# Part of the stores moved from SyncE's queue to ScalarE's

## The chip, the cores and the metric

The kernel runs on one core of a Trainium2 chip. The metric is the device time of one execution in microseconds; before the change it was 1874.4 us (median of two runs, 1874.36 and 1874.45). The core has five engines, each with its own stream of instructions: TensorE (PE, matmul), VectorE (DVE), ScalarE (ACT), GpSimd (POOL) and SyncE (SP). Here SyncE only issues DMA transfers. ScalarE can issue them too.

## The reference

The inputs are `xi` and `xj`, each 1024 samples x 39 rows x 16 numbers. For each pair of rows c < r (741 pairs) the outer product of row r of `xj` with row c of `xi` is formed, normalised over samples and elements (one mean and one variance per pair), scaled and shifted by `gamma` and `beta`, and multiplied by a 16 x 16 matrix W:

```python
cross = xj[:, rows, :, None] * xi[:, cols, None, :]          # 1024 x 741 x 16 x 16
mean = jnp.mean(cross, axis=(0, 2, 3), keepdims=True)
var = jnp.mean(jnp.square(cross - mean), axis=(0, 2, 3), keepdims=True)
normed = (cross - mean) * jax.lax.rsqrt(var + BN_EPS)
normed = normed * gamma[None, :, None, None] + beta[None, :, None, None]
out = normed[:, :, None, :, :] * W[None, None, :, :, :]
```

The output is 1024 x 741 x 256 float32, 777 MB; the inputs are 5 MB.

## The kernel before

128 partitions hold 8 samples each (NT = 8). From Gram sums the kernel first works out a scale s and a shift t for every pair, so that the output is (x * s + t) * W. Then it goes through 152 tiles. A tile is one row r with its r pairs, for T = 2 of the 8 samples. The first four tiles are row 19, the next eight alternate between rows 20 and 18. Then come the rows 38 down to 21, each together with the short row 38 - r (38 stands alone), so that a long and a short tile always fill 76 places of the buffer `y_sb`. That buffer has room for two such fillings, used in turn (`slot`).

```python
mid = (F - 1) // 2                                            # 19
tiles = [(mid, t0, t0 // T * half // 2) for t0 in range(0, NT, T)]
slot = 0
for r in (mid + 1, *range(F - 1, mid + 1, -1)):
    for t0 in range(0, NT, T):
        tiles.append((r, t0, slot * half))
        if r < F - 1:
            tiles.append((F - 1 - r, t0, slot * half + T * r))
        slot ^= 1
```

`products(n)` forms the outer products of tile n into `y_sb`: 32 instructions (2 samples x 16 numbers of `xj`), most on ScalarE, the rest on GpSimd. For rows of 7 and less (OUTER = 7) they are formed by GpSimd, and for 4 and less by VectorE, without ScalarE.

```python
for t in range(T):
    for i in range(E):
        product(n, nc.scalar if i < split else nc.gpsimd, t, i, xs[:, t])
```

`finish(n)` adds t and multiplies by W in place. VectorE does one instruction for each pair and both samples; a few pairs are GpSimd's (in rows over 33 ScalarE does the first half of that share). It is here that the stores are issued, piece by piece, as pairs become finished:

```python
for t in range(0, T, size):                                   # size = 2 from tile 2 on
    for c0, c1 in zip(bounds(n), bounds(n)[1:]):
        for c in [*range(c0, min(c1, p0)), *range(max(c0, p1), c1)]:
            stt(y[:, t : t + size, c, :], y[:, t : t + size, c, :],
                t_sb[:, n0 + c : n0 + c + 1], w_dve.to_broadcast([P, size, EE]), ALU.add, ALU.mult)
        store(n, c0, c1, t, t + size)

def store(n, c0, c1, t_from=0, t_to=T):
    r, t0, _ = tiles[n]
    n0 = first[r]
    whole = n >= len(FIRST_PIECES) and r <= WHOLE             # 8 entries; WHOLE = 36
    step = 1 if r > mid and (whole or c1 == r) else t_to - t_from
    for t in range(t_from, t_to, step):
        if whole and step == 1 and t == t_to - 1:
            if c1 < r:
                continue
            c0 = 0
        nc.sync.dma_start(
            out_v[:, t0 + t : t0 + t + step, (n0 + c0) * EE : (n0 + c1) * EE],
            view(n)[:, t : t + step, c0:c1, :].rearrange("p t n e -> p t (n e)"))
```

`bounds(n)` gives one piece for rows up to 30 and two above. So a long row up to 30 is stored as two transfers (one for each sample), a row of 31 to 36 as three (two pieces of the first sample, then the second sample whole), rows 37 and 38 as three (the first piece of both samples in one transfer, then the last piece of each sample), and a short row as one.

The loop puts the instructions into each engine's stream in this order:

```python
for n in range(1, len(tiles)):
    if n + 2 < len(tiles):
        scale_xi(n + 2)                                       # GpSimd: xi times s
    finish(n)
    ...
    if n + 1 < len(tiles):
        products(n + 1)
    ...
```

Of the kernel before, what the change touches and what calls it, by code (L numbers as in the profile page):

```python
# [14 lines left out]
T = 2  # L15
# [4 lines left out]
FIRST_PIECES = (  # L20
    (0, 1, 3, 6, 10, 14, 19), (0, 4, 9, 14, 19), (0, 4, 11, 19), (0, 9, 19), (0, 10, 20), (0, 9, 18), (0, 10, 20), (0, 9, 18)
)
# [10 lines left out]
OUTER, POOL_I_BESIDE = 7, 3  # L33
# [10 lines left out]
def tile_pair_outer_batchnorm(  # L44
# [15 lines left out]
    nc = tc.nc  # L60
# [3 lines left out]
    EE = E * E  # L64
# [7 lines left out]
    tiles = [(mid, t0, t0 // T * half // 2) for t0 in range(0, NT, T)]  # L72
# [25 lines left out]
    out_v = out.rearrange("(p t) o n i j -> p t (o n i j)", t=NT)  # L98
# [44 lines left out]
    def view(n):  # L143
        r, _, u = tiles[n]
        return y_sb[:, u : u + T * r, :].rearrange("p (t n) e -> p t n e", t=T)

    def product(n, engine, t, i, src):

        r, t0, _ = tiles[n]
        y = view(n).rearrange("p t n (i j) -> p t n i j", j=E)[:, t, :, i, :]  # L150
        scale = xj_sb[:, t0 + t, r, i : i + 1]
        if engine is nc.scalar:
            nc.scalar.activation(y, src, AF.Copy, scale=scale)  # L153
        else:
            engine.tensor_scalar(y, src, scale, 1.0, ALU.mult, ALU.mult)  # L155
# [13 lines left out]
    def scale_xi(n):  # L169
        r, t0, _ = tiles[n]  # L170
        if r <= SHORT:
            return
        n0 = first[r]
        xs = scaled.tile([P, T, r, E], F32, tag="xs", name=f"xs_{r}_{t0}")
        nc.gpsimd.tensor_tensor(  # L175
            xs,
            xi_sb[:, t0 : t0 + T, 0:r, :],
            s_sb[:, :, n0 : n0 + r, :].to_broadcast([P, T, r, E]),
            ALU.mult,
        )  # L180
        xs_of[n] = xs

    def products(n):

        r, t0, _ = tiles[n]
        if r <= SHORT:
            xs = scaled_short.tile([P, T, r, E], F32, tag="xs_short", name=f"xs_{r}_{t0}")
            nc.vector.tensor_tensor(
                xs,
                xi_sb[:, t0 : t0 + T, 0:r, :],  # L190
                s_short[:, first[r] : first[r] + r]
                .unsqueeze(1)
                .unsqueeze(3)
                .to_broadcast([P, T, r, E]),
                ALU.mult,
            )
            for t in range(T):
                nc.vector.tensor_tensor(  # L198
                    view(n)[:, t].rearrange("p n (i j) -> p n i j", j=E),
                    xs[:, t].unsqueeze(2).to_broadcast([P, r, E, E]),  # L200
                    xj_short[:, t0 + t, r - 1 : r, :].unsqueeze(3).to_broadcast([P, r, E, E]),
                    ALU.mult,
                )
            return
        xs = xs_of.pop(n)
        if r <= OUTER:
            for t in range(T):
                nc.gpsimd.tensor_tensor(  # L208
                    view(n)[:, t].rearrange("p n (i j) -> p n i j", j=E),
                    xs[:, t].unsqueeze(2).to_broadcast([P, r, E, E]),  # L210
                    xj_sb[:, t0 + t, r : r + 1, :].unsqueeze(3).to_broadcast([P, r, E, E]),
                    ALU.mult,
                )
            return
        if n < 3:
            split = E - POOL_I_FIRST[n]
        elif r > LONG:
            split = E - POOL_I_LONG
        else:
            split = E - (POOL_I_BESIDE if SHORT < F - 1 - r <= OUTER else POOL_I)  # L220
        for t in range(T):
            for i in range(E):
                product(n, nc.scalar if i < split else nc.gpsimd, t, i, xs[:, t])

    def store(n, c0, c1, t_from=0, t_to=T):
        r, t0, _ = tiles[n]
        n0 = first[r]

        whole = n >= len(FIRST_PIECES) and r <= WHOLE
# [3 lines that stand above are left out]
                if c1 < r:  # L233
                    continue
                c0 = 0
            nc.sync.dma_start(  # L236
                out_v[:, t0 + t : t0 + t + step, (n0 + c0) * EE : (n0 + c1) * EE],
                view(n)[:, t : t + step, c0:c1, :].rearrange("p t n e -> p t (n e)"),
            )

    def affine(n, pairs, engines=(nc.scalar, nc.gpsimd)):

# [11 lines left out]
    def weigh(n):  # L254

        y = view(n)
        for c0, c1 in zip(bounds(n), bounds(n)[1:]):
            affine(n, range(c0, min(c1, OWN)), (nc.vector,))
            nc.vector.tensor_tensor(  # L259
                y[:, :, c0:c1, :],  # L260
                y[:, :, c0:c1, :],
                w_dve.unsqueeze(1).to_broadcast([P, T, c1 - c0, EE]),
                ALU.mult,
            )
            store(n, c0, c1)
# [10 lines left out]
    def finish(n):  # L276


        r = tiles[n][0]
        n0 = first[r]  # L280
        y = view(n)
        long = r > LONG
        p1 = r // 2 if long else r
        if long:
            share = POOL_PAIRS_LONG
        elif RAW < n < 10:
            share = POOL_PAIRS_FIRST
        else:
            share = int(r * POOL_SHARE + 0.5) if r > SHORT else 0
        p0 = p1 - share  # L290
        step = POOL_PAIRS_LONG // 2 if long else r
        for c0 in range(p0, p1, step):
            c1 = min(c0 + step, p1)
            for c in range(c0, c1):
                t_c = t_sb[:, n0 + c : n0 + c + 1]
                if long:
                    nc.scalar.activation(y[:, :, c, :], y[:, :, c, :], AF.Identity, bias=t_c)  # L297
                else:
                    nc.gpsimd.tensor_scalar(  # L299
                        y[:, :, c, :], y[:, :, c, :], t_c, 1.0, ALU.add, ALU.mult  # L300
                    )
            nc.gpsimd.tensor_tensor(  # L302
                y[:, :, c0:c1, :],
                y[:, :, c0:c1, :],
                w_sb.unsqueeze(1).to_broadcast([P, T, c1 - c0, EE]),
                ALU.mult,
            )

        size = 1 if n == RAW else T
        for t in range(0, T, size):  # L310
            for c0, c1 in zip(bounds(n), bounds(n)[1:]):
                for c in [*range(c0, min(c1, p0)), *range(max(c0, p1), c1)]:
                    stt(  # L313
                        y[:, t : t + size, c, :],
                        y[:, t : t + size, c, :],
                        t_sb[:, n0 + c : n0 + c + 1],
                        w_dve.to_broadcast([P, size, EE]),
                        ALU.add,
                        ALU.mult,
                    )  # L320
                store(n, c0, c1, t, t + size)

    with tc.manual_schedule():
# [121 lines left out]
        for n in range(len(steps)):  # L445
# [12 lines left out]
            t0 = steps[n][0]  # L458
# [72 lines left out]
        def apply(group):  # L531
            ps, n0, n1 = spread_of[group]
            nc.vector.tensor_mul(ps[:, 1], ps[:, 1], st_sb[:, 0, n0:n1])
            if group == SHORT_GROUP:

                nc.vector.tensor_mul(ps[:, 0], ps[:, 0], st_sb[:, 0, n0:n1])
                nc.vector.tensor_copy(st_sb[:, 0, n0:n1], ps[:, 0])
            else:
                nc.vector.tensor_mul(st_sb[:, 0, n0:n1], ps[:, 0], st_sb[:, 0, n0:n1])
            nc.vector.tensor_add(st_sb[:, 1, n0:n1], ps[:, 1], st_sb[:, 1, n0:n1])  # L540
# [15 lines left out]
        for n in range(1, len(tiles)):  # L556
            if n + 2 < len(tiles):
                scale_xi(n + 2)
            finish(n)
            for group, (_, _, _, tile_of) in enumerate(ROW_GROUPS):  # L560
                if n == tile_of:
                    apply(group)
            if n + 1 < len(tiles):
                products(n + 1)
            if n == 12:
                nc.scalar.copy(xj_short, xj_sb[:, :, 1 : SHORT + 1, :])

# [27 lines left out]
```

## Time and profile before

| Engine | busy | share of the span | instructions |
|---|---|---|---|
| VectorE | 1723.0 us | 92% | 2641 |
| ScalarE | 1584.7 us | 85% | 3152 |
| GpSimd | 1552.0 us | 83% | 1650 |
| DMA, queue q1 | - | 98.2% of 16 engines | 53344 packets |

The span is 1873.1 us. The page of the profile gives the busy time of each engine, then the span in 40 slices of 46.8 us with the busy share of each in tenths, then the DMA queues. The groups below those say for one line of code and one engine how many instructions there were, their busy time in all, the mean of one, and after the second bar how long the engine was idle just before them and for what (the "releaser"). `out<-in` are names of the program, with the shapes (partitions x elements). "SPq" and "ACTq" are the parts of SyncE and ScalarE that issue transfers. A mean of one instruction includes its overlap with the next, so that a row of instructions takes a little less than count times mean.

Short rows are stored in one transfer of 256 KB for each pair, long rows at 128 KB for each pair and sample. From issue to landing a store took 2.3 us at the least, 18.4 us in the median and 27.8 us at the most.

### The profile page before, as it was taken

The numbers are of one execution on the slowest core, as the hardware profiler recorded it, in microseconds if no ns is written. First come the engines' busy times: TensorE is split into PE (matmuls) and PEld (weight loads), VectorE is DVE, ScalarE is ACT, GpSimd is POOL, SyncE is SP. The second block draws the span as 40 slices with busy tenths as digits, with TensorE's granted clock in tenths as the row PEclk, the third lists the DMA queues.
The fourth block names the chain that finished last, engine by engine and source line by source line (L and its number), as shares of the span: only waits on it lengthen the run. The fifth ranks groups of instructions, "written<-read, shape, count | busy, mean of one in ns | idle before, by whom it ended". The sixth has DMA issues, their size and how long they took to land. (4 is left out here: it accounts for less than half of the span.)

```text
span 1873.1 us, 9236 instructions
## 1 busy us (share of the span) xinstructions
PE 26.0 (1%) x130; PEld 23.2 (1%) x130; DVE 1723.0 (92%) x2641; ACT 1584.7 (85%) x3152; POOL 1552.0 (83%) x1650
## 2 busy tenths in 40 slices
PE   5000000000000000000000000000000000000000
PEld 4000000000000000000000000000000000000000
DVE  8999888899999999999999999999999999999994
ACT  8999888898888877666799999999899998989892
POOL 9999877787777788999988888888888888888882
DMA  5999999999999999999999999999999999999998
GB/s 210 390 422 422 428 426 424 427 425 424 428 424 427 425 429 422 427 425 425 417 435 425 426 431 427 424 431 426 426 431 426 430 426 429 427 428 427 428 426 355
DMA packets 54711, 783.61 MB, mean 418 GB/s; under 512 B 4720, under 2 KB 6384, under 8 KB 17520
## 3 DMA queue, kind: packets, MB, share of 16 engines
q1 hardware_dynamic: 53344, 779.72, 98.2%
q10 hardware_dynamic: 1296, 3.29, 0.5%
q14 instruction: 70, 0.57, 0.1%
q8 instruction: 1, 0.02, 0.0%
HBM read 6.00 MB, written 776.99 MB: 418 GB/s over the span
## 5 line engine op out<-in xcount | busy, mean ns | idle before, releaser
L313 DVE SCALAR_TENSOR_TENSOR y_sb<-y_sb,st_sb,w_dve 128x512 f32<-128x512 f32 (+1 forms) x2511 | 1653.1, 738 | 114.5 <-issue 99.1
L153 ACT ACTIVATE y_sb<-xs,xj_sb 128x144 f32<-128x144 f32 (+23 forms) x2930 | 1453.4, 587 | 239.1 <-DMA out_dram<-y_sb 207.7
L302 POOL TENSOR_TENSOR y_sb<-y_sb,w_sb 128x2048 f32<-128x2048 f32 (+3 forms) x155 | 517.7, 3345 | 90.0 <-ACT y_sb L297 80.4
L155 POOL TENSOR_SCALAR y_sb<-xs,xj_sb 128x320 f32<-128x320 f32 (+19 forms) x1006 | 558.3, 581 | 9.1 <-DMA out_dram<-y_sb 9.0
L175 POOL TENSOR_TENSOR xs<-xi_sb,st_sb 128x640 f32<-128x640 f32 (+33 forms) x135 | 184.1, 1363 | 179.2 <-ACT y_sb L153 174.6
L299 POOL TENSOR_SCALAR y_sb<-y_sb,st_sb 128x512 f32<-128x512 f32 x291 | 197.1, 694 | 5.1 <-ACT y_sb L153 5.1
L297 ACT ACTIVATE y_sb<-y_sb,st_sb 128x512 f32<-128x512 f32 x160 | 100.2, 709 | 3.9 <-POOL y_sb L155 2.2
L208 POOL TENSOR_TENSOR y_sb<-xs,xj_sb 128x1280 f32<-128x1280 f32 (+2 forms) x24 | 66.7, 2803 | 0.0
L198 DVE TENSOR_TENSOR y_sb<-xs,ps 128x256 f32<-128x256 f32 (+3 forms) x32 | 24.8, 818 | 0.5
L522 PE MATMUL ps<-y_sb 38*128 38x38 f32 (+37 forms) x76 | 16.4, 397 | 2.8 <-DVE y_sb L508 2.8
L522 PEld LDWEIGHTS ps<-y_sb 38*128 38x128 f32 x76 | 16.3, 329 | 3.1 <-DVE y_sb L508 3.1
L379 ACT ACTIVATE y_sb<-y_sb 128x1216 f32<-128x1216 f32 x8 | 9.7, 1211 | 2.9 <-POOL y_sb L368 2.6
L153 ACT ACTIVATE y_sb<-xi_sb,xj_sb 128x304 f32<-128x304 f32 x24 | 11.4, 538 | 0.0
L384 DVE TENSOR_REDUCE y_sb<-y_sb 128x76 f32<-128x1216 f32 (+1 forms) x9 | 10.9, 1268 | 0.0
L259 DVE TENSOR_TENSOR y_sb<-y_sb,w_dve 128x2048 f32<-128x2048 f32 (+4 forms) x6 | 10.7, 1840 | 0.1
L368 POOL TENSOR_TENSOR y_sb<-xi_sb,y_sb 128x1216 f32<-128x1216 f32 x4 | 9.0, 2262 | 1.2 <-DMA xi_sb<-in_r_xi_dram 1.0
L358 DVE TENSOR_REDUCE y_sb<-xi_sb 128x38 f32<-128x608 f32 (+1 forms) x6 | 5.9, 988 | 3.9 <-DMA xi_sb<-in_r_xi_dram 3.9
L368 POOL TENSOR_TENSOR y_sb<-xj_sb,y_sb 128x1216 f32<-128x1216 f32 x4 | 9.0, 2264 | 0.0
L252 POOL TENSOR_SCALAR y_sb<-y_sb,st_sb 128x512 f32<-128x512 f32 x8 | 6.4, 817 | 2.5 <-ACT y_sb L153 2.5
L404 PE MATMUL ps<-y_sb 128*38 128x77 f32 x48 | 8.1, 337 | 14.0 <-DVE y_sb L384 13.8
L358 DVE TENSOR_REDUCE y_sb<-xj_sb 128x38 f32<-128x608 f32 (+1 forms) x6 | 5.9, 990 | 1.3 <-DMA xj_sb<-in_r_xj_dram 1.3
L250 ACT ACTIVATE y_sb<-y_sb,st_sb 128x512 f32<-128x512 f32 x9 | 6.5, 801 | 0.2 <-ACT y_sb L153 0.2
(60 smaller groups left out, 42.8 us busy)
## 6 DMA issues: line engine op xcount, KB each, us to landing
out_dram<-y_sb SPq DMA_DIRECT2D x16, 3072.0 KB, 21.7
out_dram<-y_sb SPq DMA_DIRECT2D x20, 2432.0 KB, 12.5
out_dram<-y_sb SPq DMA_DIRECT2D x10, 4608.0 KB, 15.1
out_dram<-y_sb SPq DMA_DIRECT2D x12, 3840.0 KB, 21.0
out_dram<-y_sb SPq DMA_DIRECT2D x16, 2816.0 KB, 22.3
out_dram<-y_sb SPq DMA_DIRECT2D x12, 3584.0 KB, 23.1
out_dram<-y_sb SPq DMA_DIRECT2D x12, 3328.0 KB, 24.3
out_dram<-y_sb SPq DMA_DIRECT2D x15, 2560.0 KB, 11.9
```

What stands on the lines that cost most here:

```text
L153: nc.scalar.activation(y, src, AF.Copy, scale=scale)
L155: engine.tensor_scalar(y, src, scale, 1.0, ALU.mult, ALU.mult)
L175: nc.gpsimd.tensor_tensor(xs, xi_sb[:, t0 : t0 + T, 0:r, :], s_sb[:, :, n0 : n0 + r, :].to_broadcast([P, T, r, E]), ALU.mult,)
L198: nc.vector.tensor_tensor(view(n)[:, t].rearrange("p n (i j) -> p n i j", j=E), xs[:, t].unsqueeze(2).to_broadcast([P, r, E, E]), xj_short ...
L208: nc.gpsimd.tensor_tensor(view(n)[:, t].rearrange("p n (i j) -> p n i j", j=E), xs[:, t].unsqueeze(2).to_broadcast([P, r, E, E]), xj_sb[:, ...
L297: nc.scalar.activation(y[:, :, c, :], y[:, :, c, :], AF.Identity, bias=t_c)
L299: nc.gpsimd.tensor_scalar(y[:, :, c, :], y[:, :, c, :], t_c, 1.0, ALU.add, ALU.mult)
L302: nc.gpsimd.tensor_tensor(y[:, :, c0:c1, :], y[:, :, c0:c1, :], w_sb.unsqueeze(1).to_broadcast([P, T, c1 - c0, EE]), ALU.mult,)
L313: stt(y[:, t : t + size, c, :], y[:, t : t + size, c, :], t_sb[:, n0 + c : n0 + c + 1], w_dve.to_broadcast([P, size, EE]), ALU.add, ALU.mult,)
L358: nc.vector.tensor_reduce(total[:, t0:t1, part(x)], sources[x][:, t0:t1], AX.X, ALU.add)
L368: nc.gpsimd.tensor_tensor(devs[n % 7], sources[x][:, t0 : t0 + T], shift[:, x : x + 1, :].unsqueeze(3).to_broadcast([P, T, G, E]), ALU.sub ...
L522: nc.tensor.matmul(ps[:, :, first[r] - n0 : first[r] - n0 + r], pick[:, r - 1, :], stq[:, :, 0:r], start=True, stop=True,)
```

## The change

Some of the stores, from the ninth tile on (n >= 8), are no longer issued by SyncE but put on a list and issued by ScalarE: those of a tile's last sample, and those that store both samples at once. They are issued after `products(n + 1)`, and where the next tile's row is 7 or shorter, only after the products of the tile behind that. The intention is to use a second DMA queue beside SyncE's, with the issue at a place in ScalarE's stream where the tile should be near its end. All computing instructions are as before.

```diff
+    by_scalar = []
+
     def store(n, c0, c1, t_from=0, t_to=T):
 ...
-            nc.sync.dma_start(
-                out_v[:, t0 + t : t0 + t + step, (n0 + c0) * EE : (n0 + c1) * EE],
-                view(n)[:, t : t + step, c0:c1, :].rearrange("p t n e -> p t (n e)"),
-            )
+            to = out_v[:, t0 + t : t0 + t + step, (n0 + c0) * EE : (n0 + c1) * EE]
+            source = view(n)[:, t : t + step, c0:c1, :].rearrange("p t n e -> p t (n e)")
+            if n >= len(FIRST_PIECES) and (t == t_to - 1 or step == T):
+                by_scalar.append((to, source))
+            else:
+                nc.sync.dma_start(to, source)
 ...
             if n + 1 < len(tiles):
                 products(n + 1)
+            if n + 1 >= len(tiles) or tiles[n + 1][0] > OUTER:
+                for to, source in by_scalar:
+                    nc.scalar.dma_start(to, source)
+                by_scalar.clear()
             if n == 12:
                 nc.scalar.copy(xj_short, xj_sb[:, :, 1 : SHORT + 1, :])
```

## The prediction

> **What bounds the kernel now.** I read the page first, then the table of waits, then the timeline of one pair of tiles, then the groups of ScalarE by shape. "P" below is the forming of a tile's products by ScalarE (with a share on GpSimd), "F" its finishing by VectorE (add, times W), "D" its stores. From tile 12 on a long row of r pairs and a short one of 38 - r pairs alternate (38 stands alone), four times each; 72 is the first long tile with r = 30, 151 the last tile.
>
> ```profile
> PE 26.0 (1%) x130; PEld 23.2 (1%) x130; DVE 1723.0 (92%) x2641; ACT 1584.7 (85%) x3152; POOL 1552.0 (83%) x1650
> DMA  5999999999999999999999999999999999999998
> GB/s 210 390 422 422 428 426 424 427 425 424 428 424 427 425 429 422 427 425 425 417 435 425 426 431 427 424 431 426 426 431 426 430 426 429 427 428 427 428 426 355
> q1 hardware_dynamic: 53344, 779.72, 98.2%
> L313 DVE SCALAR_TENSOR_TENSOR y_sb<-y_sb,st_sb,w_dve 128x512 f32<-128x512 f32 (+1 forms) x2511 | 1653.1, 738 | 114.5 <-issue 99.1
> ```
>
> The DMA engines are full in every slice but the first and last, at about 426 GB/s, and a single queue (q1) holds 98.2% of them. So the stores bound the kernel. A pair (long and short, 38 pairs x 2 samples x 128 KB = 9.96 MB) takes 23.4 us. VectorE has some 8% to spare and ScalarE 15%, which isn't much: any order that makes those two take turns will pass 23.4 us at once.
>
> ```profile
> ACT y_sb L153 <- DMA out_dram<-y_sb: 207.7, 96, 6.6
> DVE y_sb L313 <- issue: 99.1, 68, 5.1
> SPq L236 <- DVE y_sb L313: 1428.4, 175, 18.4
> ```
>
> ScalarE waits 207.7 us for stores to land, as a full queue makes it. The third line matters most: SyncE stood 1428.4 us waiting for VectorE ahead of its stores. It has nothing else to do, so these waits cost nothing there. On ScalarE they would.
>
> ```profile
> 1006.98 21.82 DVE L313 SCALAR_TENSOR_TENSOR y_sb<-y_sb,st_sb,w_dve 128x512 f32<-128x512 f32 x33 [1.46 <-issue]
> ...
> 1014.48 6.98 ACT L153 ACTIVATE y_sb<-xs,xj_sb 128x464 f32<-128x464 f32 x12 [0.26 <-DMA out_dram<-y_sb]
> 1023.51 7.59 ACT L153 ACTIVATE y_sb<-xs,xj_sb 128x464 f32<-128x464 f32 x14 [2.04 <-DMA out_dram<-y_sb]
> ...
> 1023.67 5.65 SPq L236 DMA_DIRECT2D out_dram<-y_sb  x3
> ...
> 1030.57 4.04 DVE L313 SCALAR_TENSOR_TENSOR y_sb<-y_sb,st_sb,w_dve 128x512 f32<-128x512 f32 x6 [1.78 <-issue]
> ```
>
> The x33 are F of tile 80 (25 of row 29) and of tile 81 (8 of row 9). 25 of the 33 bring F(80) to 1023.5 us, and its stores leave at 1023.67. But ScalarE began P(82), the next long tile, at 1014.48, 9 us before F(80) ended. This lead lets F(82) start at 1030.57, 23.6 us after F(80).
>
> **What the Trainium skill says.** "DMA: Bandwidth & Descriptors", section "Issuing engines are not separate DMA queues": transfers from ScalarE and SyncE run on the same 16 engines, and a second issuer saves only time on the sequencer. So no bandwidth is to be won. The trace fits: one queue already fills the engines. The same page, "Anatomy of one DMA", says that DMA engines do not wait on semaphores; the issuing sequencer does, before it dispatches. The 1428.4 us of SyncE agree. "PSUM — Partial Sum Buffer", section "Engine vs sequencer instructions", calls ScalarE's queue strictly first in, first out; here this means that a store waiting for F holds back the P behind it. In the load phase below, ScalarE issues a DMA in 0.33 us between its own instructions, in program order.
>
> ```profile
> 5.70 0.33 ACTq L329 DMA_DIRECT2D xi_sb<-in_r_xi_dram  x1
> 6.74 0.20 ACT L421 ACTIVATE y_sb<-ps 128x38 f32<-128x38 f32 x1 [0.83 <-PE ps L413]
> ```
>
> **The change, part by part.** Nothing is computed more or less. Of 279 stores 152 move: 2 + 2 (tiles 8 to 11), 16 (rows 38 and 37: the second sample's last piece, and the first piece too, since it is stored with both samples in one step), 68 (short rows), 24 (rows 36 to 31), 40 (rows 30 to 21). At 0.33 to 1.3 us each (SyncE's issues have median 0.38 and longest 1.327), some 90 us of ScalarE's 239 us of idle time. That alone would be bearable. The place is what counts: D(n) stands on ScalarE behind P(n+1) and ahead of P(n+2), and it waits for the end of F(n). So P(n+2) can't start before F(n) is over, and F(n+2) can't before P(n+2) is. Only where the next row is 7 or shorter is D(n) put off until after P(n+2).
>
> *Rows 30 to 21 (tiles 72 to 151).* Step one is F(long) beside P(short), step two is P(next long) beside F(short). In both the first-named is longer (row 30: 17.1 against 7.1, and 14.3 against 4.6; row 21: 11.8 against 10.0, and 11.3 against 9.9). The pair takes F(long) + P(long). F has 26, 25, 24, 23, 23, 22, 21, 20, 19, 18 instructions on VectorE for rows 30 to 21, at 1653.1/2511 = 0.658 us; four tiles of each make 884 x 0.658 = 581.9 us. P is read from the groups by shape (16 r wide), each of four tiles:
>
> ```profile
> L153 ACT ACTIVATE y_sb<-xs,xj_sb 128x480 f32<-128x480 f32 x96 | 57.1, 681 | 14.3 <-DMA out_dram<-y_sb 14.3
> ...
> L153 ACT ACTIVATE y_sb<-xs,xj_sb 128x400 f32<-128x400 f32 x96 | 50.7, 614 | 3.3 <-DMA out_dram<-y_sb 3.3
> ...
> L153 ACT ACTIVATE y_sb<-xs,xj_sb 128x336 f32<-128x336 f32 x96 | 45.1, 562 | 0.0
> ```
>
> The ten groups are 57.1, 55.8, 54.5, 53.3, 52.0, 50.7, 49.2, 47.7, 46.4 and 45.1, in sum 511.7 us; without the first tile's 14.3, 497.4. For the handover (issue 0.33 to 1.3 us and two semaphores) I take 0.8 us a pair, 39 times: 31.2. From the start of F(72) to the end of F(150): 581.9 + 497.4 + 31.2 = 1110.5 us. Before, F(72) started at 915.05 and F(150) ended at 1835.8 in the timeline: 920.8. Loss **+190 us**: 8.5 us a pair at row 30, near none at row 21. The transfers are hidden here, as a pair has 31 us for 23.4 us of them.
>
> *Rows 38 and 37 (tiles 12 to 23).* P(next but one) needs the first piece of the same buffer landed, and this is now issued only at P(next)'s end rather than halfway through F. A tile takes 4.98 MB / 0.426 = 11.7 us for the first piece (4.72 MB, 11.1 us, in row 37), 1.5 us for issue and landing (my choice: the shortest store of all landed in 2.3 us), and P of 15.4 us (15.1): 28.6 and 27.7 us. Before it was about 23.4. Eight such tiles give 8 x 4.7 = 38 us; the first one is worse by about 5, as at the start all four parts leave together, and tiles 8 to 12 add some 3: **+45 us**.
>
> *Rows 36 to 31.* D(long) is put off behind P(next long). With both started together, F with the short row takes about 21.5 us (tile 24: 356.5 to 377.9), and P is over some 12.6 (landing of the second sample) + 7.4 = 20 us on. Both are under the 23.4 us of the transfers, which stay the bound with little queued ahead. I allow 0.4 us for each of 24 pairs: **+10 us**.
>
> *End.* Before, the last store landed 37.3 us after F(150), behind a queue of old stores. With an empty queue the last pair takes 23.4 + 2.5 us: **-11 us**.
>
> Sum: 190 + 45 + 10 - 11 = +234 us on 1874.4: about **2108 us**, 12.5% more.
>
> **The rivals.** *Issue only:* ScalarE pays 90 us for issuing, inside its idle time; the stores still bound, and the time stays at 1870 to 1880. Against it is that P(82) starts 9 us before F(80) ends, a lead that the new order forbids. *Two queues move more:* a second queue could fill gaps between transfers, and the best slice shows 435 GB/s where the mean is 418. At 435 all the way the stores would take 777 MB / 0.435 = 1786 us, and with the start some 1835 (-2%). Against it is that the engines are at 9 tenths or more already. *Rows 36 to 31 fall behind too:* a first-sample piece of the next tile shares the engines with the second sample that P waits for; then a pair takes 26 to 27 us rather than 23.8, and the total comes to some 2180.
>
> **Range and chances.** The 190 us are sums of measured durations under an order that the code fixes; uncertain are the handover (0.3 to 1.4 us, -20 to +25 us), rows 38 and 37 (25 to 65 us) and rows 36 to 31 (0 to 70 us). I predict 2108 us, with a range of 2065 to 2170. Faster by over 2%: 0.02; within 2%: 0.03; slower by over 2%: 0.95. The small chances are for my having misread what the store waits for.
>
> **What would show it.** In the profile after: DMA at 7 to 8 tenths in the second half of the slices, rising to 9 at the end, and ScalarE waiting some 8 us for VectorE once a pair at row 30, near nothing at row 21. F(80) to F(82) should be about 31 us apart and P(82) should start right behind F(80). The groups' mean times should stay as they are. In the stretch of rows 36 to 31 DMA should stay at 9 tenths; if it falls there, the third rival is right. If DMA stays full throughout, the main step is wrong.

## The result and the profile after

The changed kernel takes 2131.0 us (two runs, 2130.95 and 2131.11) against 1874.4: 1.137 times as long, with a 95% interval of 1.134 to 1.140. The predicted time was 2108 us, the range 2065 to 2170. In the page of the changed kernel these lines answer to those shown of before (a line number has moved: `stt` in `finish` is now L317):

```profile
PE 26.0 (1%) x130; PEld 23.2 (1%) x130; DVE 1722.2 (81%) x2641; ACT 1579.3 (74%) x3152; POOL 1550.7 (73%) x1650
DMA  6998888999999888888767877787788888999999
GB/s 236 394 425 369 374 371 378 426 391 408 404 411 394 375 374 374 375 374 375 325 287 325 343 313 323 331 373 335 340 342 356 351 373 375 387 387 401 405 417 401
q10 hardware_dynamic: 33168, 476.21, 52.8%
q1 hardware_dynamic: 21472, 306.81, 34.0%
L317 DVE SCALAR_TENSOR_TENSOR y_sb<-y_sb,st_sb,w_dve 128x512 f32<-128x512 f32 (+1 forms) x2511 | 1652.1, 738 | 382.4 <-issue 360.5
```

No engine works longer than before (VectorE 1722.2 us, the mean of its main instruction still 738 ns). What has grown is idle time: VectorE's before that instruction from 114.5 to 382.4 us. Two queues, q1 (SyncE's) and q10 (ScalarE's), now share the DMA engines, and together fill 87% of them instead of 98%. The slices from the 20th on, where row 30 begins, fall to 287 to 343 GB/s and climb back to over 400 at the end.

The table of waits of the changed kernel (engine, line, waited for, us in all, times, longest):

```profile
DVE y_sb L317 <- issue: 360.5, 60, 11.9
ACT y_sb L153 <- DVE y_sb L317: 293.1, 36, 20.5
ACT y_sb L153 <- DMA out_dram<-y_sb: 116.0, 13, 19.6
```

ScalarE waited mostly for stores to land before; now it waits 293.1 us for VectorE. Of these, 236.9 us fall in rows 30 to 21. The three longest (56.3 us, in rows 33 to 31) only bear VectorE's name: they are waits for stores, as the section on rows 38 to 31 shows. The pair of tiles whose timeline was shown above looks like this in the changed kernel:

```profile
1125.63 21.82 DVE L317 SCALAR_TENSOR_TENSOR y_sb<-y_sb,st_sb,w_dve 128x512 f32<-128x512 f32 x33 [9.85 <-issue]
...
1142.29 0.37 ACTq L571 DMA_DIRECT2D out_dram<-y_sb  x1
1142.33 0.33 SPq L243 DMA_DIRECT2D out_dram<-y_sb  x1
1142.71 7.55 ACT L153 ACTIVATE y_sb<-xs,xj_sb 128x464 f32<-128x464 f32 x13 [9.84 <-DVE y_sb L317]
...
1156.64 4.04 DVE L317 SCALAR_TENSOR_TENSOR y_sb<-y_sb,st_sb,w_dve 128x512 f32<-128x512 f32 x6 [9.19 <-issue]
```

F(80) starts at 1125.63 and its 25 instructions end at 1142.2. Only then does ScalarE issue the store (1142.29), and only then, after 9.84 us of idling, does it begin P(82) (1142.71). F(82) can't start before that P is done, at 1156.64: 31.0 us after F(80), where it was 23.6. VectorE in its turn idles 9.19 us.

Following the starts of F through the timelines of both kernels, the 256.3 us between the two profiled spans (2129.4 and 1873.1) split as follows:

| Stretch | predicted | measured |
|---|---|---|
| start to F(24): rows 20, 18, 38, 37 | +45 us | +23.4 us (of them +3.0 to F(12)) |
| F(24) to F(72): rows 36 to 31 | +10 us | +59.5 us |
| F(72) to the end of F(150): rows 30 to 21 | +190 us | +184.2 us (1105.0 after 920.8) |
| end of F(150) to the end | -11 us | -10.9 us (26.4 after 37.3) |

So the main term held. The two smaller ones did not: one was about twice what it came to, the other a sixth of it. Their errors (-21.6 and +49.5 us) have opposite signs, so that the sum came out only 23 us under the measured time; that part is luck. The runs below ask two questions: whether the turns of ScalarE and VectorE are the cause in rows 30 to 21, and what the cause is before them. "Late" below is always against the kernel before at the start of the same F.

### The profile page after: what moved, and what is told of

It is laid out like the page before. It is cut to its first block, busy times and chain, and to the rows that moved or that the text cites. A ratio compares the mean times of both kernels' runs of the same rounds, so it can differ in the third digit from the quotient of the medians.

```text
span 2129.4 us, 9038 instructions
## 1 busy us (share of the span) xinstructions
PE 26.0 (1%) x130; PEld 23.2 (1%) x130; DVE 1722.2 (81%) x2641; ACT 1579.3 (74%) x3152; POOL 1550.7 (73%) x1650
## 5 line engine op out<-in xcount | busy, mean ns | idle before, releaser
L317 DVE SCALAR_TENSOR_TENSOR y_sb<-y_sb,st_sb,w_dve 128x512 f32<-128x512 f32 (+1 forms) x2511 | 1652.1, 738 | 382.4 <-issue 360.5
L153 ACT ACTIVATE y_sb<-xs,xj_sb 128x144 f32<-128x144 f32 (+23 forms) x2930 | 1447.9, 586 | 502.3 <-DVE y_sb L317 293.1
L301 ACT ACTIVATE y_sb<-y_sb,st_sb 128x512 f32<-128x512 f32 x160 | 100.2, 708 | 11.1 <-DVE y_sb L317 5.4
L388 DVE TENSOR_REDUCE y_sb<-y_sb 128x76 f32<-128x1216 f32 (+1 forms) x9 | 10.9, 1268 | 0.0
```

The source lines that it names most:

```text
L317: stt(y[:, t : t + size, c, :], y[:, t : t + size, c, :], t_sb[:, n0 + c : n0 + c + 1], w_dve.to_broadcast([P, size, EE]), ALU.add, ALU.mult,)
```

## Experiments in rows 30 to 21

**Two halves.** Only the condition in `store` changes.

```diff
-            if n >= len(FIRST_PIECES) and (t == t_to - 1 or step == T):
+            if n >= 72 and (t == t_to - 1 or step == T):                        # only_rows_30_21
+            if len(FIRST_PIECES) <= n < 72 and (t == t_to - 1 or step == T):    # only_rows_20_31
```

> Only the stores of tiles 72 to 151 (rows 30 to 21) go to ScalarE, all others stay with SyncE. Theory A (turns: a store on ScalarE that waits for F(long) keeps P of the next long row from starting): F(72) starts as in the kernel before (915 us), from there to the end of F(150) it takes 1105 us as in the changed kernel, and the tail is 11 us shorter, so about 1874 + 184 - 11 = 2047 us. Theory B (the loss comes from two queues sharing the DMA engines, in proportion to the bytes that go through ScalarE): somewhat over half of the 257 us, as this part holds 40 of the 68 tile pairs: about 2020 us, with DMA at 9 tenths. The two differ mainly in whether DMA is idle a quarter of the time at row 30.

> The complement: only tiles 8 to 71 (rows 20 to 31) go to ScalarE. If the two parts add up: F(72) starts about 83 us late (998 us) and nothing is won back later, so 1874 + 83 = 1957 us. If the later part absorbs some of the delay, as the queue of stores is then shorter: 1930 us or less.

Measured: 2046.7 us (ratio 1.092, 1.090 to 1.094) and 1957.7 us (1.044, 1.043 to 1.046). In the first, F(72) is on time (-0.5 us) and from there to the end of F(150) it takes 1104.6 us. In the second, F(72) is 82.8 us late and all that follows is 82 us late: nothing is won back. The parts add up, 172 + 83 = 255 us.

**The wait without the store.** All stores by SyncE, but ScalarE waits at the same places.

```diff
+            nc.sync.dma_start(to, source)
             if n >= len(FIRST_PIECES) and (t == t_to - 1 or step == T):
-                by_scalar.append((to, source))
-            else:
-                nc.sync.dma_start(to, source)
+                by_scalar.append(view(n)[:, t, c0:c1, 0])
 ...
-                for to, source in by_scalar:
-                    nc.scalar.dma_start(to, source)
+                for source in by_scalar:
+                    nc.scalar.copy(ps_s[:, 256 : 256 + source.shape[1]], source)
```

> All stores by SyncE; at each place where the changed kernel issues a store on ScalarE stands a copy of one element of each pair of that tile into a spare place of PSUM, which waits for the same instructions and costs some 0.2 us. It adds 152 small copies and takes the second queue away. Theory A: rows 30 to 21 take as long as in the changed kernel, 1105 us from F(72) to the end of F(150). Theory B: they take 921 us as before. For rows 38 to 31: if the second queue is what costs there (the first sample's pieces have to share the engines with the second sample and the short row, so that both land late), F(72) is late by under 25 us; if the order alone costs, by 83 us. By A and sharing together the total is 2050 to 2075 us.

Measured: 2038.4 us (1.088, 1.086 to 1.089). F(72) is 2.3 us late; from there to the end of F(150) it takes 1093.7 us, where theory A had 1105. With both stretches shorter than expected, the total lies under the 2050 to 2075 us. The timeline of ScalarE around the same tiles shows the small copy where the store stood:

```profile
1043.77 7.43 ACT L153 ACTIVATE y_sb<-xs,xj_sb 128x144 f32<-128x144 f32 x24
1060.51 0.21 ACT L570 COPY ps<-y_sb 128x29 f32<-128x29 f32 x1 [9.31 <-DVE y_sb L316]
1060.66 13.84 ACT L153 ACTIVATE y_sb<-xs,xj_sb 128x464 f32<-128x464 f32 x24
```

P(81) is done, the copy stands 9.31 us waiting for F(80), and P(82) follows. So with one queue alone 172.9 of the 184.2 us are lost again: in rows 30 to 21 the turns are the cause. The remaining 11.3 us are 0.29 us a pair, and the handover accounts for them: from the end of F(long) to the start of P(next long) the median of the 39 pairs is 0.53 us with the store between them (in the changed kernel) and 0.25 us with the copy. In rows 38 to 31, on the other hand, the same waits cost 2.3 us instead of 83. There the waits are not the cause; what is left is the second queue, or stores that leave later, and the runs further down tell these apart.

**Which store makes them take turns.**

```diff
+            if n >= 72 and r > mid and (t == t_to - 1 or step == T):            # long_rows_30_21
+            if n >= 72 and r <= mid and (t == t_to - 1 or step == T):           # short_rows_30_21
```

> In rows 30 to 21 only the long row's second sample goes to ScalarE; the short rows, and all tiles before 72, are SyncE's. Theory A: D(long) alone keeps P(next long) from starting before F(long) ends, so nothing is won by taking the short rows away: 2047 us less what the 40 short stores cost to issue and wait, 2035 to 2047 us. Theory B (cost by bytes in the second queue): these are 27% of the pair's bytes where it was 50 to 73%, so about half the loss, 1950 us.

> The complement in rows 30 to 21: only the short rows go to ScalarE, all of the long rows through SyncE. D(short) stands behind P(next long), and F(short), which follows F(long) at once, is over about when that P ends; so it makes nobody take turns. Theory A: 1870 to 1885 us. Theory B: the bytes in the second queue are 21% (row 30) to 45% (row 21) of a pair, so a loss of about half of the 172 us, 1950 us.

Measured: 2046.8 us (1.092, 1.090 to 1.094) and 1874.6 us (1.000, 0.999 to 1.001). The long row's store alone costs all of it, and the short row's store costs nothing, though in row 21 some 45% of a pair's bytes (34 of 76 places) pass through ScalarE's queue in that run. This too speaks against a cost by bytes.

**One tile later.**

```diff
+            if n >= 72 and (t == t_to - 1 or step == T):
+                by_scalar.append((n, to, source))
 ...
-            if n + 1 >= len(tiles) or tiles[n + 1][0] > OUTER:
-                for to, source in by_scalar:
+            due = n - 1 if n + 1 < len(tiles) else n
+            for m, to, source in by_scalar:
+                if m <= due:
                     nc.scalar.dma_start(to, source)
-                by_scalar.clear()
+            by_scalar[:] = [x for x in by_scalar if x[0] > due]
```

> In rows 30 to 21 the stores of tile n stand behind P(n+2) on ScalarE instead of behind P(n+1); the rows before are SyncE's. The same bytes go through the second queue. Theory A: F(n) is over when ScalarE comes to the store, nobody takes turns, and the time is 1865 to 1900 us. Theory B: the second queue costs as much as in the run with rows 30 to 21 alone, 2020 us and more.

Measured: 1892.2 us (1.009, 1.008 to 1.011). The same stores in the same queue, one place further back, cost 18 us instead of 172. What is left arises in rows 30 to 28 (F(96) is 24.1 us late, F(144) 21.9), with waits of ScalarE for stores to land. That fits what the next section shows, but no run took it apart.

## Experiments in rows 38 to 31

Here the copies in place of the stores cost almost nothing, so taking turns isn't the cause. The timeline of the changed kernel in row 31 (F(64) from 892.5 to 910.4 us) shows what ScalarE waits for:

```profile
910.49 4.30 ACTq L571 DMA_DIRECT2D out_dram<-y_sb  x2
...
930.68 9.09 ACT L153 ACTIVATE y_sb<-xs,xj_sb 128x496 f32<-128x496 f32 x15 [20.50 <-DVE y_sb L317]
```

P(68), which takes the place of tile 64 in the buffer, starts at 930.68 after 20.5 us of idling. The profile names VectorE, but F(64) had long ended; the instruction's other semaphores are those of stores. The transfers issued from 908.5 to 920 us (KB and us from issue to landing):

```profile
out_dram<-y_sb ACTq DMA_DIRECT2D x1, 3968.0 KB, 18.5
out_dram<-y_sb SPq DMA_DIRECT2D x1, 3072.0 KB, 13.5
out_dram<-y_sb ACTq DMA_DIRECT2D x1, 1792.0 KB, 19.7
out_dram<-y_sb SPq DMA_DIRECT2D x1, 896.0 KB, 20.2
```

The first sample's small rest (7 pairs, 896 KB), issued at 910.45, lands 20.2 us later, at 930.61, just ahead of P(68). The same holds throughout rows 36 to 31: wherever P waits for a store in its first instruction, from P(28) to P(72), it starts within 0.15 us of the landing of such a rest. In the window from 921.4 to 928.3 us, while it is being moved, the two queues stand thus (packets, MB, share of the engines):

```profile
q10 hardware_dynamic: 94, 2.14, 72.5%
q1 hardware_dynamic: 109, 0.78, 27.0%
```

The rest is in q1, SyncE's queue. A packet here is one partition's row: 7 KB (0.27 us) of the rest against 31 KB (1.18 us) of the second sample in the other queue. The numbers of packets are about equal, the bytes are not. "DMA: Bandwidth & Descriptors" of the Trainium skill says in "Queues, rings and completion order" that a DMA engine goes round the queues packet by packet. The packet records of this trace agree. Where they follow one another without a gap, they make up 16 sequences, as many as there are engines, and from 921.6 to 927.3 us every sequence takes a 7 KB row and a 31 KB row in turn. So theory C: a queue of short rows starves beside one of long rows.

**Rows 36 to 31 alone, and the rest moved.**

```diff
+            if 24 <= n < 72 and (t == t_to - 1 or step == T):                   # rows_36_31
+            if 24 <= n < 72 and (t == t_to - 1 or step == T or c0 > 0):         # rows_36_31_rest_first
```

> Only rows 36 to 31 (tiles 24 to 71) with their second sample and short rows on ScalarE, as in the change; all others SyncE's. In the changed kernel this stretch lost 59 us. Expected the same here, 1930 us (1920 to 1935), of which rows 33 to 31 lose about 12 us a row and rows 35 and 34 about 5.

> As the run before, but the second piece of the first sample goes to ScalarE too, ahead of the second sample. Theory C (each DMA engine takes one packet in turn from either queue, and a packet is one partition's row: the second piece with its 4 to 7 pairs sends 7 KB rows against the 32 KB rows of the second sample, so it lands some 20 us after its issue, and the whole next P waits for it): in ScalarE's own queue the piece is first, it lands early, and rows 33 to 31 lose under 5 us a row; the total is 1885 to 1905 us. Theory D (the stores are late because of their place behind P): still later or the same, 1930 us or more.

Measured: 1932.2 us (1.031, 1.029 to 1.033) and 1874.1 us (0.9998, 0.999 to 1.001). The second is below the 1885 to 1905 us that theory C was given. (The rest has 17 pairs in row 36 and 7 in row 31, not 4 to 7.) One more store on ScalarE's queue takes away the whole loss, though the second sample and the short row stay there, behind P as they were. That refutes lateness by place.

**The second sample in short rows.**

```diff
-                by_scalar.append((to, source))
+                width = (c1 - c0) * EE
+                cut = 8 * EE if step == 1 else width
+                for e in range(0, width, cut):
+                    stop_e = min(e + cut, width)
+                    by_scalar.append((to[:, :, e:stop_e], source[:, :, e:stop_e]))
```

> As the run with rows 36 to 31 alone, same queues, places and bytes, but the second sample is stored in pieces of at most 8 pairs, so that its rows are 8 KB or less instead of 32 KB; this adds 3 or 4 issues a tile on ScalarE (0.4 us each, 1.6 us of some 8 us of slack). Theory C (one packet in turn from either queue, a packet being a row): the first sample's second piece, eight 7 KB packets on each DMA engine, then waits 8 x 0.31 us for the other queue's packets instead of 8 x 1.19, and lands some 7 us earlier; that takes the next P forward by 7 us in every second pair, and the loss of 57 us falls to 0 to 20, a total of 1874 to 1895 us. If the DMA engines shared by bytes, or if the piece is late for another reason, the loss stays at 57 us, or grows by the added issues: 1930 us and more.

Measured: 1897.0 us in the median (1888.9 to 1897.6; 1.012, 1.010 to 1.014), so 22 us are left of 57, slightly more than theory C allowed. The profile is of the fastest of the four executions (1888.9 us), in which 15 us were left. The four stores of the first sample's rest in row 31 show it in the list of DMA issues (KB each, median us from issue to landing). In the run with rows 36 to 31 alone:

```profile
out_dram<-y_sb SPq DMA_DIRECT2D x4, 896.0 KB, 18.0
```

With the second sample cut:

```profile
out_dram<-y_sb SPq DMA_DIRECT2D x4, 896.0 KB, 13.9
```

With the rest first, in ScalarE's queue:

```profile
out_dram<-y_sb ACTq DMA_DIRECT2D x4, 896.0 KB, 10.9
```

And in the kernel before the change:

```profile
out_dram<-y_sb SPq DMA_DIRECT2D x4, 896.0 KB, 11.1
```

18.0 us beside 31 KB rows, 13.9 beside 8 KB rows, 10.9 in front of them in the same queue, 11.1 in the kernel before. The order of the losses is the same: 57, 15 (in this profile), 0 and 0 us. The cut has side effects that this run doesn't separate: 3 or 4 more issues a tile, and pieces may leave before their sample's last pairs are done. So it supports theory C, and what makes up the 22 us, and why one execution was 8 us faster, stays open.

**Rows 38 and 37.** Here the rows of both queues are equally long (19 KB), and I had put the loss down to the first piece leaving late.

```diff
+            if 12 <= n < 24 and t == t_to - 1:                                  # rows_38_37_last_piece
+            if 12 <= n < 24 and c0 > 0:                                         # rows_38_37_rest_first
```

> Only rows 38 and 37, and of them only the second sample's last piece goes to ScalarE; the first piece of both samples stays with SyncE and leaves halfway through F as before. In the changed kernel this stretch lost 20 us (F(12) 3.0 us late, F(24) 23.4 us). Theory E (the loss is the late issue of the first piece, which the next but one P needs whole): the loss falls to 0 to 5 us, a total of 1874 to 1879 us. Theory F (a second sample on the second queue is enough for it): 15 to 20 us remain, 1890 us and more.

> Only rows 38 and 37: the first piece of both samples stays with SyncE, the last pieces of both samples go to ScalarE, the first sample ahead of the second. More bytes in the second queue than in the run with the second sample's piece alone. Theory C, widened (what costs is that the two samples' pieces lie in different queues, so that they land together, at the time of the last, while in one queue the first sample's lands some 6 us earlier and the next P can begin on it): the loss of 20 us falls to 0 to 5, a total of 1874 to 1880 us. If the second queue costs by itself, the loss stays or grows: 1896 us and more.

Measured: 1896.0 us (1.012, 1.010 to 1.013), F(24) 20.0 us late; and 1874.1 us (0.9999, 0.999 to 1.001), F(24) on time. So the first piece's late issue is not needed for the loss: with it back in its place, the loss is the same. It vanishes once the last pieces of both samples are in one queue again. The stores of the run with the second sample's last piece alone in the second queue, from 171 to 356 us:

```profile
out_dram<-y_sb SPq DMA_DIRECT2D x7, 2432.0 KB, 16.6
out_dram<-y_sb ACTq DMA_DIRECT2D x7, 2432.0 KB, 16.3
```

They leave within 3 us of each other and land within 1.4 us of each other. In the kernel before, tile 12's last pieces went out at 190.8 and 191.2 us, and P(14) began at 201.7 on the first one's landing:

```profile
201.74 15.34 ACT L153 ACTIVATE y_sb<-xs,xj_sb 128x608 f32<-128x608 f32 x22 [4.19 <-DMA out_dram<-y_sb]
```

In this run both went out at 191.1, and P(14) began at 207.8: 6 us later, the time of one such piece (2.49 MB at 426 GB/s).

```profile
207.76 7.73 ACT L153 ACTIVATE y_sb<-xs,xj_sb 128x608 f32<-128x608 f32 x11 [10.02 <-DMA out_dram<-y_sb]
```

In the changed kernel itself two delays lie over each other. There the first piece is in ScalarE's queue, and in six of the eight P's that wait here (P(15), 18, 20, 22, 24 and 26) it lands last, just ahead of P. P(15) begins so, on the landing at 233.15 of a first piece issued at 217.80:

```profile
233.23 2.19 ACT L153 ACTIVATE y_sb<-xs,xj_sb 128x608 f32<-128x608 f32 x3 [2.10 <-DMA out_dram<-y_sb]
```

In four of the six the first sample's last piece lands less than 1 us before it; in P(15) and P(18) it had landed 11.6 and 9.8 us before. P(14) and P(16) start on the first sample's last piece. No run has the late first piece alone, so what it would cost by itself stays open.

**Everything in order.**

```diff
+            rest = c0 > 0 or (n >= 24 and (t == t_to - 1 or step == T))
+            if (12 <= n < 72 and rest) or (n >= 72 and r <= mid):
```

> Everything that the runs left without a loss, put together: rows 38 to 31 with the last pieces of both samples on ScalarE in their order (and the short rows of 36 to 31), rows 30 to 21 with the short rows alone there; rows 20 and 18 with SyncE. As the DMA engines are full all the time in the kernel before, a second queue can win nothing and this gives 1870 to 1882 us. If two queues fill the engines better, it is 1855 us or less.

Measured: 1874.6 us (1.0001, 0.9993 to 1.001), with q10 holding 43.7% of the DMA engines and q1 55.1%. None of the runs beats the kernel before.

## Why the prediction was right, and where it was not

*What bounds the kernel.* Right: the stores fill the engines, and no arrangement of two queues got below 1874 us in the median. With everything in order the time is the same within 0.1%, so the rival "two queues move more" is refuted for this kernel. The section "Issuing engines are not separate DMA queues" of the Trainium skill's "DMA: Bandwidth & Descriptors" says the same.

*Rows 30 to 21.* Right in mechanism and size: 1105.0 us where 1110.5 were predicted. F and P as measured before (581.9 and 497.4 us) leave 25.7 us for 39 handovers: 0.66 us each, where I chose 0.8. (The gaps read from the trace are 0.53 us from F to P and 0.09 us from P to F.) Shown by the run that waits without storing and by the two runs with long and short rows alone. The rival "issue only" falls with them.

*Rows 38 and 37.* The term of 45 us was too high (23.4), and half of the mechanism was missing. P does wait for the first piece, as predicted, in six of the eight tiles. The step that failed is "this is now issued only at P(next)'s end", with 12.6 us from there to the landing. In the changed kernel the first piece leaves some 8 us before that P ends (last section), and then takes longer, as it shares the engines with the other queue. That of tile 18 (row 37) left at 320.90, 7.0 us after P(20) began, and landed 18.5 us later, so that P(22) began 25.6 us after P(20), where 27.7 were predicted. What was missing: the two samples' last pieces in different queues land together, at the time of the later one, while one queue lets P begin on the first. By itself this makes F(24) 20.0 us late.

*Rows 36 to 31.* The term of 10 us was too low (59.5). The step that failed is "P is over some 12.6 (landing of the second sample) + 7.4 = 20 us on". It watched the second sample only and took the first to have landed long before. In fact all four parts of a pair leave within 6 us (908.56 to 914.41 in row 31), and of those that P waits for the first sample's rest lands last. The second sample landed 18.5 us after its issue instead of 12.6, the rest at 20.2; all of P(68) had to wait for it and was over 35.9 us after that issue (910.49 and 946.36), not 20. The third rival foresaw the sharing and 26 to 27 us a pair; in row 31 it is 26.4 us (F(64) at 892.5, F(72) at 998.0, four pairs). But it had the wrong part waiting.

*End.* Right, 26.4 us for 25.9. The signs named for it were there: DMA at 6 to 8 tenths rising to 9, ScalarE's wait for VectorE falling from 10.9 us a pair at row 30 to 2.7 at row 21 (some 8 and near nothing were named), P(82) right behind F(80), unchanged means. DMA in rows 36 to 31 did not stay full, which pointed to the third rival.

*The sum.* Its small slips (the ten groups of P add to 511.8 us, and 38 + 5 + 3 is 46) change nothing. The range held because it left 0 to 70 us for rows 36 to 31.

## What to carry to other kernels

In this kernel a DMA issue waited in the stream of the engine that issues it. Put on a computing engine, it held back everything behind it (9.84 us before P(82)), so ask when the data it waits for is ready and what stands behind. A second queue added no bandwidth where one filled the engines (1874.6 us against 1874.3), but it gave up an order: two stores that one queue landed 10.8 and 17.1 us after their issue (tile 12) both took 16.6 us in two queues, and a store of 7 KB rows beside 31 KB rows took 20.2 us, where it took 11.1 in one queue. Keep stores whose landing is awaited in sequence in one queue, and let only those go to another that nothing waits for soon, as the short rows here (1874.6 us).

## What the runs showed of the hardware

ScalarE's issuing part runs ahead of its computing part. The changed kernel in row 38, timeline of ScalarE:

```profile
217.80 1.72 ACTq L571 DMA_DIRECT2D out_dram<-y_sb  x2
218.32 7.71 ACT L153 ACTIVATE y_sb<-xs,xj_sb 128x608 f32<-128x608 f32 x11
226.12 5.01 ACT L301 ACTIVATE y_sb<-y_sb,st_sb 128x512 f32<-128x512 f32 x8
```

The two stores stand behind the 22 instructions of P(14) in program order, but are issued at 217.80, with 11 of them still to start and 8.2 us before the last ends. At row 31 it was again 11 instructions and 7.1 us (939.28 against 946.4). Of the 152 stores that ScalarE issues in the changed kernel, 44 left with 11 instructions of the P ahead of them not yet begun, and none with more. So a store that has nothing else to wait for left up to 8.2 us earlier than its place suggests.
